# Eight transformer layers on one core: a planned order of short steps, scores computed twice, weights multiplied first

## The chip, the cores and the metric

The kernel runs on one core of a Trainium2 chip. The metric is device time in microseconds (us) for one execution of the whole program. All arithmetic is float32. Five engines matter: PE (TensorE, matmuls; PEld is its weight load), DVE (VectorE), ACT (ScalarE), POOL (GpSimd) and SP (SyncE, which only issues transfers here). Each engine works through its own instructions in order.

## The reference

The input is 8 sequences of 256 tokens with 128 features. Eight residual layers follow each other, each on a layernormed copy of x:

```python
x = x + causal_attention(ln(x))        # 1 head, key size 64: softmax(q k^T / 8) (x w_v1) w_v2
x = x + ffn_relu(ln(x))                # only expert 0 counts; ends in a layernorm of its own
x = x + linear_attention(ln(x))        # (theta phi^T) g / sqrt(128), no softmax; latent size 32
x = x + ffn_relu(ln(x))
x = x + retention(ln(x))               # 16 heads of 8, values of 16, decaying causal mask, gate
x = x + ffn_silu(ln(x))                # hidden 384, weights from int32 times 1/127
x = x + softmax_attention(ln(x))       # 16 heads of 8, weights with a low-rank part, no mask
x = x + ffn_silu(ln(x))
```

A sequence needs no other sequence. In softmax attention each of the 16 heads has scores of 256 x 256, with only 8 numbers in each dot product.

## The kernel before, in words

The 2048 tokens are cut into four groups of 512 (two sequences each), and a group into four tiles of 128 tokens. x stays in SBUF for the whole kernel (tiles `x0` to `x3`). All weights are loaded at the start; those for later layers stand behind x in the SP queue.

Every layer of a group is a Python generator that yields at a few places. A small loop at the end of `hybrid` keeps two layers of two different groups active and advances them in turn; since layers are handed out group by group, the four groups go through one layer two at a time before the next layer begins. The order on an engine is the order in which the generators were advanced, as the tile framework then places it. Buffers come from rotating pools of two to four; PSUM is three pools of two buffers: `ps_two` (two banks each), `ps_one` and `ps_held` (one bank each). A new tile waits until the last user of the buffer's former tile is done.

Places that the change and the prediction touch:

- `layernorm` (L204 to L217): statistics per tile on DVE, variance plus epsilon on DVE (L216), power -0.5 on POOL (L217), four normalisations on DVE (L209). `transposed` (L237, L239): four transposes on PE, one copy out on ACT.
- `causal_attention` (L261 to L313): q, k, v1 projections, value product, scores (L280), exponential (L291), transposes (L299), weighted values (L304 to L308).
- `ffn_relu`: L361 up, L362 and L365 the relu on ACT and DVE, L375 down, L369, L248 and L383 biases and scale on POOL. `ffn_silu`: L598 gate, L599 up, L600 silu, L607 down.
- `linear_attention` (L322 to L345): theta, phi and g projections, then phi^T g, then the product with theta.
- `spread_heads` (L391): one DMA per head moves its 8 rows of q and k to a partition group of 32[...].
- `retention`: projections L437 and L451, chunk scores L470 (64x64 pieces), states L486 to L499, carried part L514, weighted values L522 (64x17 pieces), root on DVE (L222 to L231), gate L551, output L557 to L567. `centre_values` (L185, L186) prepares a weight.
- `softmax_attention`, for each of 64 pairs of heads, in a pipeline of three: `probabilities` with queries as rows (L642), maxima over a row on DVE (L648), four exponentials with the maximum as a bias per row (L654); `turned`, eight transposes (L667) and two copies out (L671), because the next product needs keys as rows; `weighted` (L401), values with a column of ones, which yields the sums as well. After four pairs the result is turned back (L410, L414) and divided (L684, L685).

Of the kernel before, what the change touches and what calls it, by code (L numbers as in the profile page):

```python
# [10 lines left out]

# [25 lines left out]
ONES = 16  # L37
EPS = 1e-5
MASKED = -1e30
PAIRS = [(b, h2) for b in range(2) for h2 in range(HEADS // 2)]  # L40
HEADS_NEXT = "heads"
# [3 lines left out]
def hybrid(ctx: ExitStack, tc: tile.TileContext, t: dict, out: bass.AP):  # L45
    nc = tc.nc

    const = ctx.enter_context(tc.tile_pool(name="const", bufs=1))
    work = ctx.enter_context(tc.tile_pool(name="work", bufs=2))
    work3 = ctx.enter_context(tc.tile_pool(name="work3", bufs=3))  # L50
    small = ctx.enter_context(tc.tile_pool(name="small", bufs=4))
    psum = ctx.enter_context(tc.tile_pool(name="psum", bufs=2, space=bass.MemoryType.PSUM))

    def two_banks():
        return psum.tile([P, 2, N], F32, tag="two", name="ps_two")

    def one_bank():
        return psum.tile([P, N], F32, tag="one", name="ps_one")

    def held_bank():  # L60
        return psum.tile([P, N], F32, tag="held", name="ps_held")


    def load(name, shape, src=None, dtype=F32):
        tl = const.tile(shape, dtype, tag=name, name=f"c_{name}")
        nc.sync.dma_start(tl, t[name] if src is None else src)
        return tl

    def load_row(name, n):

        tl = const.tile([P, n], F32, tag=name, name=f"c_{name}")
        nc.scalar.dma_start(tl, t[name].partition_broadcast(P))
        return tl
# [4 lines left out]
    for g in range(GROUPS):  # L78
        x.append(const.tile([P, NT, D], F32, tag=f"x{g}", name=f"x{g}"))
    nc.sync.dma_start(x[0], x_in[0])  # L80
    w_qkv1 = load("a_qkv1", [P, 3, 64])
    for g in range(1, GROUPS):
        nc.sync.dma_start(x[g], x_in[g])
    w_v2 = load("a_v2", [64, D])
    w1 = load("f_w1", [P, 512])
    w2 = load("f_w2", [P, 4, D], t["f_w2"].rearrange("(c p) d -> p c d", p=P))
    w_tpg = load("b_tpg", [P, 192])
    w_ret_qk = load("r_qk", [P, 4, P])
    rot_tab = load("r_tab", [P, 4, S])
    w_ret_vg = load("r_vg", [P, 512])  # L90
    w_ret_o = load("r_o", [P, 2, D], t["r_o"].rearrange("(c p) d -> p c d", p=P))
# [7 lines left out]
    b1 = const.tile([P, 4], F32, tag="f_b1", name="c_f_b1")  # L99
# [4 lines left out]
    b_ret_qk = const.tile([P, 4], F32, tag="r_qkb", name="c_r_qkb")  # L104
# [6 lines left out]
    ident = const.tile([P, P], F32, tag="ident", name="ident")  # L111
    make_identity(nc, ident)
    minus_half = const.tile([P, 32], F32, tag="mhalf", name="mhalf")
    nc.gpsimd.memset(minus_half, -0.5)

    causal_add = const.tile([P, 3, P], F32, tag="causal_add", name="causal_add")
    nc.gpsimd.memset(causal_add, 0.0)

    causal_mul = const.tile([P, 1, P], F32, tag="causal_mul", name="causal_mul")
    nc.gpsimd.memset(causal_mul, 1.0)  # L120
    for c in (0, 2):
# [4 lines left out]
    nc.gpsimd.affine_select(  # L126
        out=causal_mul[:, 0, :], in_=causal_mul[:, 0, :], compare_op=ALU.is_ge,
        fill=0.0, base=0, pattern=[[1, P]], channel_multiplier=-1,
    )

    chunk_mul = const.tile([P, 64], F32, tag="chunk_mul", name="chunk_mul")
    for e in range(2):
        half = slice(64 * e, 64 * e + 64)
        nc.gpsimd.tensor_copy(chunk_mul[half, :], causal_mul[half, 0, half])
    causal_add = causal_add.rearrange("p a b -> p (a b)")

    own_head = const.tile([P, HEADS, VONE], F32, tag="own_head", name="own_head")
    nc.gpsimd.memset(own_head, 1.0)
    for step, base in ((-KDIM, 0), (KDIM, KDIM - 1)):
        nc.gpsimd.affine_select(  # L140
            out=own_head, in_=own_head, compare_op=ALU.is_ge, fill=0.0, base=base,
            pattern=[[step, HEADS], [0, VONE]], channel_multiplier=1 if base == 0 else -1,
        )


    values32 = []
    for g in range(2):
        values32.append(const.tile([P, NT, HEADS, 32], F32, tag=f"v{g}", name=f"values32_{g}"))
        nc.gpsimd.memset(values32[g], 1.0)


    def dequantised(wi, shape, name):
        w = const.tile(shape, F32, tag=name, name=name)
        nc.vector.tensor_copy(w, wi)
        nc.vector.tensor_scalar_mul(w, w, float(np.float32(1.0 / 127.0)))
        return w

    def prepare_ffn_int():
        return (
            dequantised(wi_gate, [P, 384], "wf_gate"),  # L160
            dequantised(wi_up, [P, 384], "wf_up"),
            dequantised(wi_down, [P, 3, D], "wf_down"),
        )

    def prepare_lora():

        w = w_lora
        ps = one_bank()
        for i in range(3):
            nc.tensor.matmul(  # L170
                ps[:, i * P : (i + 1) * P], lora_a[:, i, :], lora_b[:, i, :], start=True, stop=True
            )
        nc.vector.scalar_tensor_tensor(
            w.rearrange("p i d -> p (i d)"), ps[:, : 3 * P], 2.0,
            w_lora.rearrange("p i d -> p (i d)"), ALU.mult, ALU.add,
        )
        nc.vector.tensor_scalar_mul(w[:, 0, :], w[:, 0, :], float(KDIM**-0.5))
        return w

    def centre_values():  # L180

        for w in (w_ret_vg, b_ret_vg):
            v = w[:, : HEADS * VDIM].rearrange("p (h d) -> p h d", h=HEADS)
            mean = const.tile([P, HEADS], F32, tag="r_mean", name="r_mean")
            nc.vector.tensor_reduce(mean, v, AX.X, ALU.add)  # L185
            nc.vector.scalar_tensor_tensor(  # L186
                v, spread_over(mean, VDIM), -1.0 / VDIM, v, ALU.mult, ALU.add
            )

# [8 lines left out]
    def layernorm(src):  # L198
        stats = small.tile([P, NT, 6], F32, tag="ln_stats", name="ln_stats")
        mv = small.tile([P, NT, 2], F32, tag="ln_mv", name="ln_mv")  # L200
        rstd = small.tile([P, NT], F32, tag="ln_rstd", name="ln_rstd")
        y = work3.tile([P, NT, D], F32, tag="ln_y", name="ln_y")
        for i in range(NT):
            nc.vector.bn_stats(stats[:, i, :], src[:, i, :])  # L204
            nc.vector.bn_aggr(mv[:, i, :], stats[:, i, :])  # L205
        inverse_root(rstd, mv[:, :, 1], 1.0)
        yield
        for i in range(NT):
            nc.vector.tensor_scalar(  # L209
                y[:, i, :], src[:, i, :], mv[:, i, 0:1], rstd[:, i : i + 1], ALU.subtract, ALU.mult  # L210
            )
        return y

    def inverse_root(rstd, var, scale):

        nc.vector.tensor_scalar(rstd, var, scale, EPS, ALU.mult, ALU.add)  # L216
        nc.gpsimd.tensor_tensor(rstd, rstd, minus_half[:, : rstd.shape[1]], ALU.pow)  # L217

    def newton_root(r, a):

        t = small.tile(list(a.shape), F32, tag="root_t", name="root_t")
# [11 lines left out]
    def transposed(y):  # L233

        ps = one_bank()
        for i in range(NT):
            nc.tensor.transpose(ps[:, i * P : (i + 1) * P], y[:, i, :], ident)  # L237
        yT = work3.tile([P, N], F32, tag="yT", name="yT")
        nc.scalar.copy(yT, ps)  # L239
        yield  # L240
        return yT

    def normalised(g):
        y = yield from layernorm(x[g])
        return (yield from transposed(y))

    def add_row_to(g, row):
        nc.gpsimd.tensor_tensor(x[g], x[g], tokens(row, NT), ALU.add)  # L248

    def add_to(g, tiles, ps):  # L250
        xs = flat(x[g][:, tiles, :])
        nc.vector.tensor_tensor(xs, ps, xs, ALU.add)  # L252


    def causal_attention(g):
        yT = yield from normalised(g)
        qk = work.tile([64, 2, N], F32, tag="a_qk", name="a_qk")
        v1T = work.tile([64, N], F32, tag="a_v1T", name="a_v1T")
        ps = two_banks()
        for i in range(2):  # L260
            nc.tensor.matmul(ps[:64, i, :], w_qkv1[:, i, :], yT, start=True, stop=True)  # L261
        nc.vector.tensor_copy(qk, ps[:64])
        ps = one_bank()
        nc.tensor.matmul(ps[:64, :], w_qkv1[:, 2, :], yT, start=True, stop=True)
        nc.scalar.copy(v1T, ps[:64, :])
        yield
        values = work.tile([P, NT, D], F32, tag="values", name="a_values")
        ps = one_bank()
        for i in range(NT):
            nc.tensor.matmul(  # L270
                ps[:, i * P : (i + 1) * P], v1T[:, i * P : (i + 1) * P], w_v2, start=True, stop=True
            )
        nc.scalar.copy(flat(values), ps)
        yield
        for b in range(2):
            at = b * S
            blocks = ((0, 0, P), (P, P, 3 * P))
            ps = one_bank()
            for q0, lo, hi in blocks:
                nc.tensor.matmul(  # L280
                    ps[:, lo:hi], qk[:, 0, at + q0 : at + q0 + P], qk[:, 1, at : at + hi - lo],
                    start=True, stop=True,
                )
# [308 lines left out]
    def ffn_silu(g, w_gate, w_up, w_down):  # L592
        yT = yield from normalised(g)
        hT = work.tile([P, 3, N], F32, tag="hT", name="g_hT")
        for c in range(3):
# [6 lines left out]
            if c > 0:  # L602
                yield
# [238 lines left out]
```

## Time and profile before

| | |
|---|---|
| time, median of 3 runs | 765.78 us (765.4 to 773.27) |
| span in the profile | 772.2 us, 12437 instructions |
| granted TensorE clock, mean | 0.829 |
| transfers | 10.49 MB, mean 14 GB/s |

| stage, by the chain of waits | us from the start |
|---|---|
| loads, first layernorms | 0 to 19 |
| causal attention | 19 to 72 |
| feed-forward (relu) | 72 to 129 |
| linear attention | 129 to 152 |
| feed-forward (relu) | 152 to 213 |
| retention | 213 to 422 |
| feed-forward (silu), softmax attention, feed-forward (silu) | 422 to 772 |

The profile page lists busy time per engine, then forty equal slices of the span with the busy share in tenths, then the chain of work that ended last, followed back from the last instruction. Groups of instructions have a line, an engine, an operation, output<-input, sizes, count, busy time and mean duration of one, then the idle time ahead of them and what ended it. "Clock" is the share of PE's full clock that the chip granted. These are the costliest groups:

```profile
L654 ACT ACTIVATE l_p<-ps_two,l_nmax 128x256 f32<-128x256 f32 x256 | 100.5, 475 | 108.1 <-DVE l_nmax L648 108.1
L648 DVE TENSOR_REDUCE l_nmax<-ps_two 128x4 f32<-128x1024 f32 x64 | 78.3, 1223 | 41.1 <-PE ps_two L642 40.1
L217 POOL TENSOR_TENSOR ln_rstd<-ln_rstd,mhalf 128x4 f32<-128x4 f32 x40 | 40.6, 1016 | 415.8 <-DVE ln_rstd L216 415.8
L671 DVE COPY l_pT<-ps_held 128x512 f32<-128x512 f32 x128 | 82.6, 676 | 9.3 <-PE ps_held L667 9.2
L642 PE MATMUL ps_two<-spread 8*128 8x256 f32 x512 | 79.4, 404 | 0.3 <-DMA spread<-qk 0.3
L667 PE MATMUL ps_held<-ident,l_p 128*128 128x128 f32 x512 | 74.6, 282 | 0.8 <-ACT l_p L654 0.8
```

### The profile page before, as it was taken

Reading aid. Unit: us, or ns where it says so; the run is one execution under the profiler, and the core shown is the slowest. Engines: PE = TensorE matmul, PEld = TensorE weight load, DVE = VectorE, ACT = ScalarE, POOL = GpSimd, SP = SyncE. Lnnn points to the kernel's source line nnn. Section 1 sums busy time; section 2 is a strip of 40 time slices with the busy share of each in tenths; the row PEclk is TensorE's granted clock in tenths of the full one; section 3 lists DMA queues with packets and bytes.
Section 4 is the critical chain, followed back from the end, with each engine's and each line's share of the span. In section 5 each row is a group of like instructions: output and inputs, shape, how many; then the busy total and the mean of one; then the engine's idle time right before and its main releaser. Section 6 shows DMA issues by size and latency. Waiting matters only on the chain.

```text
span 772.2 us, 12437 instructions
## 1 busy us (share of the span) xinstructions
PE 653.3 (85%) x5038; PEld 421.3 (55%) x5038; DVE 436.2 (56%) x1120; ACT 215.7 (28%) x468; POOL 108.1 (14%) x107
## 2 busy tenths in 40 slices
PE   0989574984588979989889978999999999999985
PEld 0556443662433865655556655666666666565653
DVE  3662546645583445434533455588688688766542
ACT  0333120221010011100100222544454454456541
POOL 5021233324251010110110022100000000000000
PEclk9875867995876556757655899899999999999997
DMA  7000000000003000010010000210010010000000
GB/s 227 4 1 0 1 0 1 1 0 0 1 10 45 3 1 2 12 18 2 12 18 2 2 0 1 40 16 1 1 28 2 1 28 1 1 14 1 15 14 14
DMA packets 10232, 10.49 MB, mean 14 GB/s; under 512 B 1776, under 2 KB 8512, under 8 KB 10176
## 3 DMA queue, kind: packets, MB, share of 16 engines
q1 hardware_dynamic: 9024, 9.11, 5.9%
q10 hardware_dynamic: 1152, 0.59, 0.4%
q8 instruction: 40, 0.66, 0.3%
q14 instruction: 16, 0.13, 0.1%
HBM read 4.45 MB, written 1.05 MB: 7 GB/s over the span
## 4 chain that ended last, share of the span: by engine, by line
PE 72%; DVE 15%; POOL 5%; ACT 3%; DMA 2%; issue 2%; POOLq 0%; ACTq 0%; SPq 0%; DVEq 0%
PE ps_two L642 9%; PE ps_one L401 8%; PE ps_held L667 8%; PE ps_held L522 5%; PE ps_two L361 4%; PE ps_one L495 4%; PE ps_two L470 3%; DVE ln_y L209 3%; POOL ln_rstd L217 3%; PE ps_one L607 2%; PE ps_one L237 2%; PE ps_two L598 2%; PE ps_two L437 2%; PE ps_two L599 2%; PE ps_one L375 2%; PE ps_one L567 2%
## 5 line engine op out<-in xcount | busy, mean ns | idle before, releaser
L654 ACT ACTIVATE l_p<-ps_two,l_nmax 128x256 f32<-128x256 f32 x256 | 100.5, 475 | 108.1 <-DVE l_nmax L648 108.1
L648 DVE TENSOR_REDUCE l_nmax<-ps_two 128x4 f32<-128x1024 f32 x64 | 78.3, 1223 | 41.1 <-PE ps_two L642 40.1
L217 POOL TENSOR_TENSOR ln_rstd<-ln_rstd,mhalf 128x4 f32<-128x4 f32 x40 | 40.6, 1016 | 415.8 <-DVE ln_rstd L216 415.8
L237 PE MATMUL ps_one<-ident,ln_y 128*128 128x128 f32 x128 | 31.3, 377 | 71.6 <-DVE ln_mv L205 42.3
L671 DVE COPY l_pT<-ps_held 128x512 f32<-128x512 f32 x128 | 82.6, 676 | 9.3 <-PE ps_held L667 9.2
L642 PE MATMUL ps_two<-spread 8*128 8x256 f32 x512 | 79.4, 404 | 0.3 <-DMA spread<-qk 0.3
L667 PE MATMUL ps_held<-ident,l_p 128*128 128x128 f32 x512 | 74.6, 282 | 0.8 <-ACT l_p L654 0.8
L401 PE MATMUL ps_one<-l_pT,values 128*32 128x256 f32 x512 | 73.3, 385 | 0.0
L667 PEld LDWEIGHTS ps_held<-ident,l_p 128*128 128x128 f32 x512 | 56.9, 142 | 24.0 <-ACT l_p L654 13.6
L237 PEld LDWEIGHTS ps_one<-ident,ln_y 128*128 128x128 f32 x128 | 19.9, 176 | 84.3 <-issue 54.7
L642 PEld LDWEIGHTS ps_two<-spread 8*128 8x128 f32 x512 | 48.3, 185 | 26.8 <-issue 20.3
L239 ACT COPY yT<-ps_one 128x512 f32<-128x512 f32 x32 | 18.8, 587 | 137.5 <-PE ps_one L237 137.3
L209 DVE TENSOR_SCALAR ln_y<-x,ln_mv,ln_rstd 128x128 f32<-128x128 f32 x128 | 45.2, 398 | 20.7 <-POOL ln_rstd L217 20.6
L522 PEld LDWEIGHTS ps_held<-values,r_s 64*64 64x64 f32 x1024 | 46.4, 188 | 6.0 <-issue 5.2
L522 PE MATMUL ps_held<-values,r_s 64*64 64x17 f32 x1024 | 48.0, 243 | 0.0
L252 DVE TENSOR_TENSOR x<-ps_one,x 128x256 f32<-128x256 f32 (+1 forms) x28 | 15.0, 536 | 48.2 <-PE ps_one L567 21.5
L470 PEld LDWEIGHTS ps_two<-spread 8*64 8x64 f32 x1024 | 27.9, 187 | 26.3 <-issue 19.1
L401 PEld LDWEIGHTS ps_one<-l_pT,values 128*32 128x32 f32 x512 | 27.4, 109 | 26.3 <-issue 12.7
L470 PE MATMUL ps_two<-spread 8*64 8x64 f32 x1024 | 35.6, 290 | 5.0 <-DVE r_s L475 5.0
L495 PE MATMUL ps_one<-values,r_k 64*128 64x272 f32 (+1 forms) x64 | 33.2, 640 | 4.0 <-ACT r_k L488 4.0
L204 DVE BATCH_NORM_STATS2 ln_stats<-x 128x6 f32<-128x128 f32 x128 | 31.7, 272 | 7.9 <-DMA x<-in_x 7.6
L361 PE MATMUL ps_two<-yT,c_f_w 128*128 128x512 f32 x64 | 34.4, 690 | 0.0
(144 smaller groups left out, 893.9 us busy)
## 6 DMA issues: line engine op xcount, KB each, us to landing
spread<-qk SPq DMA_DIRECT2D x128, 32.0 KB
x<-in_x SPq DMA_DIRECT2D x4, 256.0 KB
out<-x SPq DMA_DIRECT2D x4, 256.0 KB
c_f_w<-in_f_w SPq DMA_DIRECT2D x2, 256.0 KB
c_r_tab<-in_r_tab SPq DMA_DIRECT2D x1, 512.0 KB
c_r_vgb<-in_r_vgb ACTq DMA_DIRECT2D x1, 256.0 KB
c_r_qk<-in_r_qk SPq DMA_DIRECT2D x1, 256.0 KB
c_r_vg<-in_r_vg SPq DMA_DIRECT2D x1, 256.0 KB
```

The lines of the kernel that those rows point to most:

```text
L209: nc.vector.tensor_scalar(y[:, i, :], src[:, i, :], mv[:, i, 0:1], rstd[:, i : i + 1], ALU.subtract, ALU.mult)
L237: nc.tensor.transpose(ps[:, i * P : (i + 1) * P], y[:, i, :], ident)
L361: nc.tensor.matmul(ps[:, k, :], w1[:, c * P : (c + 1) * P], yT, start=True, stop=True)
L401: nc.tensor.matmul(o[32 * i : 32 * (i + 1), (j % 2 + 1) * S - weights.shape[1] : (j % 2 + 1) * S], v, weights, start=(n == 0), stop=(n == ...
L470: nc.tensor.matmul(ps[64 * e : 64 * e + 64, k, 64 * jt : 64 * jt + 64], heads[rows, jt // 2, 1, at : at + 64], heads[rows, jt // 2, 0, at ...
L495: nc.tensor.matmul(ps[:, : HEADS * VONE], k[:rows, m, :], v[:rows, 2 * b + m, :, :VONE], start=(c == 0), stop=(c == len(pieces) - 1),)
L522: nc.tensor.matmul(ps[half, VONE * h : VONE * (h + 1)], s[half, h % 4, h // 4 * 2 + m, :], v[half, 2 * b + m, h, :VONE], start=alone, stop ...
L642: nc.tensor.matmul(ps[:, k, m * S : (m + 1) * S], qk[rows, j, 0, at + m * P : at + (m + 1) * P], qk[rows, j, 1, at : at + S], start=True, ...
L648: nc.vector.tensor_reduce(nmax, ps.rearrange("p k (m s) -> p (k m) s", m=2), AX.X, ALU.max, negate=True)
L654: nc.scalar.activation(p[:, k, m * S : (m + 1) * S], ps[:, k, m * S : (m + 1) * S], AF.Exp, bias=nmax[:, 2 * k + m : 2 * k + m + 1],)
L667: nc.tensor.transpose(ps[:, c * S + m * P : c * S + (m + 1) * P], p[:, k, m * S + c * P : m * S + (c + 1) * P], ident,)
L671: nc.vector.tensor_copy(flat(pT[:, 2 * k : 2 * k + 2, :]), ps)
```

## The change

**Threads and a plan.** Each group is one thread that runs through all eight layers; inside a layer it spawns further threads for independent parts. A thread asks for buffers from stores (8 PSUM banks, 31 work buffers and some others), names steps ("this engine, this many us"), and emits the instructions of a step when its turn comes. A planner inside the kernel walks through these steps at build time with the durations written in the kernel, gives each engine the earliest step that can start (the lower group first where several can), and so fixes the order of each engine and the use of each buffer. The framework then keeps that order (`manual_schedule`). Some copies, normalisations and relus may go to ACT or DVE, whichever the plan finds free first.

**Scores twice.** Instead of turning the probabilities, the kernel computes the scores a second time with keys as rows. The maximum of each query enters the second product as a ninth row of the operands (the maximum on the query side, ones on the key side), so that one exponential covers a pair of heads without a bias, and its result feeds the weighted values as it is. The maxima get there by a transpose, a copy and a DMA. The first scores of one pair and the second of another are issued together, where possible on four different row groups.

**Weights multiplied first.** W_q W_k^T and W_v1 W_v2 are made once, as is the product of phi and theta; linear attention then starts from y^T y.

**Smaller edits.** Layernorm computes a shift beside the root on POOL, so that ACT can normalise; heads are stored so that one DMA moves four of them; retention's states come from chunks of 64, summed on POOL; the int weights are converted in place; the output leaves in halves.

Core of the diff (lines that are only "..." mark what is left out):

```diff
-    def turned(p):
-        pT = work.tile([P, 4, S], F32, tag="l_pT", name="l_pT")
-        for k in range(2):
-            ps = held_bank()
-            for c in range(2):
-                for m in range(2):
-                    nc.tensor.transpose(...)
-            nc.vector.tensor_copy(flat(pT[:, 2 * k : 2 * k + 2, :]), ps)
-        return pT
...
+    def pairs_of_scores():
...
+            yield step(PE, 0.9)
+            for n in range(2):
+                for k in range(2):
+                    if one:
+                        seq, h2 = one
+                        rows, j = place(2 * h2 + k)
+                        nc.tensor.matmul(
+                            ps1[:, k, n * S : (n + 1) * S],
+                            seq.spread[rows, j, 0, n * P : (n + 1) * P],
+                            seq.spread[rows, j, 1, :], start=True, stop=True,
+                        )
+                    if two:
+                        seq, h2 = two
+                        rows, j = place(2 * h2 + k)
+                        nc.tensor.matmul(
+                            ps2[:, k, n * S : (n + 1) * S],
+                            seq.spread[rows, j, 1, n * P : (n + 1) * P],
+                            seq.spread[rows, j, 0, :], start=True, stop=True,
+                        )
...
+    def maxima(seq, h2, ps):
...
+        for j in range(2):
+            yield step(SP, 0.5)
+            nc.sync.dma_start(
+                seq.spread[KDIM:P:32, 2 * half + j, 0, :], rows[8 * j : 8 * j + 8, :]
+            )
...
+    def exponentials(seq, h2, ps):
+        p = yield get(probs)
+        yield step(ACT, 1.05, "exp")
+        nc.scalar.activation(flat(p), flat(ps), AF.Exp)
...
     def layernorm(src, y):
...
-        inverse_root(rstd, mv[:, :, 1], 1.0)
+        yield step(POOL, 1.5)
+        nc.gpsimd.tensor_scalar(rstd, mv[:, :, 1], EPS, None, ALU.add)
+        nc.gpsimd.tensor_scalar(shift, mv[:, :, 0], -1.0, None, ALU.mult)
+        nc.gpsimd.tensor_tensor(rstd, rstd, minus_half, ALU.pow)
+        nc.gpsimd.tensor_tensor(shift, shift, rstd, ALU.mult)
...
+    for g in range(GROUPS):
+        plan.start(layers(g), g, 4.0 + 1.5 * g)
...
+    plan.run()
...
-        hybrid(tc, t, out)
+        with tc.manual_schedule():
+            hybrid(tc, t, out)
```

## The prediction

> **What bounds the kernel now.** I read the engine totals and the slices first, then the chain of waits, then the chain in the softmax stage, then the timeline of the start.
>
> ```profile
> PE 653.3 (85%) x5038; PEld 421.3 (55%) x5038; DVE 436.2 (56%) x1120; ACT 215.7 (28%) x468; POOL 108.1 (14%) x107
> PE   0989574984588979989889978999999999999985
> PEclk9875867995876556757655899899999999999997
> PE 72%; DVE 15%; POOL 5%; ACT 3%; DMA 2%; issue 2%; POOLq 0%; ACTq 0%; SPq 0%; DVEq 0%
> ```
> TensorE carries 72% of the chain. From 480 us on it is busy in nearly every slice; between 213 and 422 us (retention) it is busy at a low clock; before that it has gaps.
>
> ```profile
> 501.12 1.07 PE ps_two L642 x8
> 502.19 1.02 PE ps_held L667 x8
> 503.22 0.99 PE ps_one L401 x8
> 504.21 1.07 PE ps_two L642 x8
> ```
> This is the chain in the softmax stage, nothing but TensorE. One pair of heads costs 504.21-501.12 = 3.09 us: scores, transposes, weighted values. 64 pairs: 198 us. (A float32 matmul is two instructions here, a transpose one.)
>
> ```profile
> 266.33 3.53 PE ps_held L522 x64
> 433.87 1.97 PE ps_held L522 x64
> 238.00:300.00 62.00, 55.74 (x654) 38.71 (x653) 20.20 (x58) 5.62 (x14) 3.59 (x3) 0.51 0.07 11
> 494.00:560.00 66.00, 65.82 (x486) 41.86 (x484) 50.40 (x81) 31.65 (x78) 1.02 (x1) 1.00 0.07 10
> 72.00:129.00 57.00, 35.74 (x176) 23.89 (x174) 28.55 (x106) 7.84 (x12) 18.61 (x16) 0.80 0.00 1
> ```
> The same 64 instructions of retention take 3.53 us at the half clock and 1.97 at the full one. The windows (busy PE, PEld, DVE, ACT, POOL; clock last but two) show retention's core at 0.51, softmax at 1.00 and 99.7% busy, and the first feed-forward layer only 63% busy on TensorE: two groups at a time do not hide a layernorm's chain DVE-POOL-DVE-PE-ACT there.
>
> ```profile
> 17.56 0.42 DVE L185 TENSOR_REDUCE r_mean<-c_r_vg 128x16 f32<-128x256 f32 x1 [4.03 <-DMA c_r_vg<-in_r_vg]
> 19.20 2.27 PE L237 MATMUL ps_one<-ident,ln_y 128*128 128x128 f32 x8 [19.20 <-DVE ln_y L209]
> ```
> TensorE starts at 19.2 us because VectorE, in order, waits for a late weight of retention ahead of the first normalisation.
>
> [...] The trace has two side by side: a 512-column matmul costs 0.86 us (chain: L437 x4 in 1.73), so four 256-column ones in series would be 1.72; L642's eight instructions take 1.07. Four at once it does not show. [...] Here 4 x 0.216 = 0.86 of the 1.07 is streaming, so I charge 0.2 us a change. [...]
>
> **The change part by part**, with instruction counts from the built order of the changed kernel.
>
> *Softmax.* Per pair it drops 8 transposes (1.02 us PE), two 128x512 evictions on DVE (L671: 128 x 676 ns = 83 us in all), and turns four exponentials of 128x256 (475 ns each, 100.5 us in all) into one of 128x1024; the nearest row is Silu L457, 1058 ns, so 64 x 1.06 = 68 us. It adds a second score product per pair, keys as rows. First and second scores of different pairs are issued together, over four row groups where both are at hand. The built order has 39 such double steps, 25 with first scores alone and 25 with second alone: 89 steps. A double step has twice the instructions over twice the row groups, so I take the measured 1.07 us for each kind: 89 x 1.07 = 95 us. Bounds: with no gain from four groups a double step costs 0.86 more, 34 us in all. Weighted values go over four column groups instead of two: 32 blocks of 16 instructions at the 0.99 us of L401's eight = 32 us (60 if they gain nothing). So 127 us against 198. The maximum travels to the second product through a transpose, a copy and one DMA (32 in all; chain: "483.38 2.40 DMA spread<-qk"). Since TensorE runs in order, a late row holds all matmuls queued behind it, those of other groups too; I put 0 to 1 us on each, 0 to 32, and take 0 because the order leaves other steps between.
>
> *Weights multiplied first.* Causal attention loses two of its three 512-column projections per group, and the 64x1024 copy (1.21 us); linear attention works on y'y. About 10 us less on PE, contained in the counts below.
>
> *Layernorm.* The DVE step L216 (7.1 us) goes; 107 of 160 normalisations move to ACT; POOL has four instructions instead of one (pow 1.02 us; the others I take at 0.1 to 0.2, from memsets of 0.1), so the POOL leg grows from 1.0 to about 1.5 us: 40 times, but hidden where three other groups run.
>
> *TensorE's sum, at full clock.* 124 matmuls of 512 columns x 0.865 = 107. 390 of 128 columns x 0.224 (L375 x32 in 3.59) = 87, and 8 of 256, 3. 296 transposes x 0.128 (L667 x8 in 1.02) = 38. Retention's small ones: scores 16 x 1.91 = 31; weighted values 16 x between 1.97 and 3.53, I take 2.75, = 44; states and carried parts 48 matmuls x 0.63 (L495 x4 in 1.32; L514 x2 in 0.60) = 30. Softmax 127. The built order changes tile shape 255 times, of which 121 are inside the softmax prices; 134 x 0.2 = 27. Sum 494 us, against 653 busy before.
>
> *The other engines*, at before's durations: DVE keeps the statistics (64) and the maxima (78) and has about 90 in retention; all rows together 343 us instead of 436. ACT rises to about 250, with 22 table loads x 1.28 instead of 16. POOL 141. None reaches TensorE, so these edits cost nothing where TensorE has work queued.
>
> *Threads.* Four groups instead of two are interleaved in steps, over 8 PSUM banks and 31 work buffers held singly. So one group's layernorm lies beside another's matmuls. Before, TensorE was busy 652.5 of the 753 us after its start, 87%, with 99.7% in the softmax stage and 63% in the worst. I take 94%: 494/0.94 = 526 us. The retention weights no longer stand in front of the first normalisation; x[0] is there at 3.71 us and ACT is free of its DMA issues at 8.2, so TensorE starts near 9 us instead of 19. The end needs about 4 us after the last matmul, as now. 526 + 9 + 4 = 539, say 540 us.
>
> **Rivals.**
>
> A. Narrow tiles gain nothing from four groups, and retention, now spread over more of the span, drags the rest into the half clock. PE 494 + 34 + 28 + 13 (weighted values all cold) + 25 (a tenth of the 250 us of wide matmuls and transposes cold) = 594; at 92% 646 + 13 = 659. For it: clock 0.51 over retention's core though TensorE is 90% busy there. Against: [...] softmax at clock 1.00 with 8-row matmuls.
>
> B. Retention runs beside dense work and stays warm (weighted values 32 us, states 20): 494 - 22 = 472, at 97% 487 + 9 + 4 = 500. For it: 99.7% in softmax before with only two groups. Against: the first 100 us of TensorE's work (causal, linear, feed-forward) have as much on DVE, by my sum 104 us, so TensorE cannot be full there.
>
> C. The frozen order is wrong. It rests on durations fixed in the kernel; where TensorE is at half clock or a DMA late, each engine waits in order and the waits spread. At the fill of the worst window, 63%: 494/0.63 + 13 = 797, slower than before. For it: 32 DMAs on the path of the scores, every engine in order. Against: the stage with an unmixed, steady order filled TensorE[...].
>
> **How the numbers follow.** The main case 0.60, A 0.15, B 0.20, C 0.05. The time is the main case's, 540. The range reaches down past B, to 470 (468 of PE work at 100% would be about there), and up to 640, most of the way to A; outside lie C and about half of A on one side and a little of B on the other. Even A is faster by 14%: faster 0.95, same 0.01, slower 0.04.
>
> **What would show it.** Right: PE busy near 490; a double score step at about 1.1 us for 16 instructions in the chain; no transposes of probabilities; DVE near 343 with L671's copies gone; first matmul near 9 us; clock above 0.85; the chain still led by PE. Wrong: double steps near 1.9 us or clock below 0.75 (A); PE waits on the rows' DMA, or PE fill below 80% with waits spread over all engines (C); DVE at over 85% of the span would mean that I priced the evictions or the normalisations too low.

## The result: 568 us, and the profile after

| | before | changed |
|---|---|---|
| time, median of 4 runs each | 768.75 us | 568.1 us (559.82 to 572.31) |
| ratio | | 0.7329, 95% interval 0.7213 to 0.7445 |
| span in the profile | 772.2 us | 565.8 us |
| PE busy, and without work | 653.3, 118.9 us | 506.0, 59.8 us |
| granted TensorE clock, mean | 0.829 | 0.891 |

The ratios here and below leave the slower runs of a kernel out, so they need not be the quotient of the medians, and the profiles of the paired steps and of the third twin are of such slower runs. The forecast was 540 us, range 470 to 640; the time lies inside, 28 us above the forecast. Of the 206 us that the span lost, 147 are work and 59 idle time of TensorE. No run separates saved work from the higher clock in the 147; as an estimate, busy time times mean clock falls from 653.3 x 0.829 = 542 to 506.0 x 0.891 = 451, so some 90 us would be saved work.

The page of the changed kernel, in the same places as before: totals, slices and the engines of the chain.

```profile
PE 506.0 (89%) x5020; PEld 333.5 (59%) x5020; DVE 328.9 (58%) x877; ACT 242.1 (43%) x426; POOL 150.6 (27%) x250
PE   2899979989999979999999999999898989677757
PEclk9999979969799698999999999995999687768768
PE 75%; DVE 12%; ACT 6%; issue 2%; DMA 2%; POOL 1%; ACTq 0%; POOLq 0%; DVEq 0%
```

TensorE does almost the same number of instructions (5020 for 5038) in 147 us less. Read the slices from both ends: from the second on they are 7 to 9, where before the first third fell to 4 and 5. The last six fall to 5 to 7, and the clock is 6 to 8 in the last nine. Before, the end was the best part; now it is the worst.

The costliest groups, those that stand against the ones shown of before:

```profile
L1035 DVE TENSOR_REDUCE small<-twin 128x4 f32<-128x1024 f32 x64 | 78.1, 1220 | 46.4 <-PE twin L1015 33.5
L1066 ACT ACTIVATE probs<-twin 128x1024 f32<-128x1024 f32 x64 | 65.5, 1023 | 77.3 <-PE twin L1015 77.0
L1082 PE MATMUL bank<-probs,l_values 128*32 128x256 f32 x512 | 40.1, 456 | 0.2 <-ACT probs L1066 0.2
L843 PE MATMUL bank<-r_values,work 64*64 64x17 f32 x768 | 30.0, 216 | 0.0
```

The maximum costs what it did (1220 ns, before 1223). One exponential of 1023 ns stands for four of 475, the transposes and their copies are gone, and the weighted values take 40.1 us instead of 73.3. L843 are retention's weighted values (another 256 write a twin).

The timeline of TensorE shows a double step of scores: start, duration, instruction.

```profile
320.28 0.48 PE L1007 MATMUL twin<-l_spread 32*128 32x256 f32 x1
320.29 0.48 PE L1015 MATMUL twin<-l_spread 32*128 32x256 f32 x1
320.30 0.48 PE L1007 MATMUL twin<-l_spread 32*128 32x256 f32 x1
320.30 0.48 PE L1015 MATMUL twin<-l_spread 32*128 32x256 f32 x1
320.60 0.37 PE L1007 MATMUL twin<-l_spread 32*128 32x256 f32 x1
...
321.36 1.13 PE L939 MATMUL bank<-work,c_g_gate 128*128 128x512 f32 x2
```

Four instructions, two of the first product (L1007) and two of the second (L1015), start within 0.02 us of each other; the next four follow at 320.60. The sixteen of the step are out of the way in 321.36 - 320.28 = 1.08 us, at a clock of 1.00. Before, eight took 1.07. That four row groups cost no more than two was my estimate in the prediction; here it is measured. As an estimate, eight 256-column products in series would be 8 x 0.43 = 3.46 us (half of the 0.865 us of a 512-column one each), so the step takes 3.2 times less.

The windows of the changed kernel (busy PE, PEld, DVE, ACT, POOL; clock last but two) tell a full stretch from the end:

```profile
300.00:350.00 50.00, 48.82 (x487) 29.11 (x485) 35.75 (x77) 33.22 (x42) 10.25 (x17) 1.00 0.11 18
400.00:450.00 50.00, 46.40 (x386) 28.81 (x385) 23.82 (x50) 27.12 (x33) 5.85 (x10) 0.86 0.03 7
450.00:500.00 50.00, 39.76 (x238) 22.66 (x236) 19.66 (x31) 13.62 (x21) 1.66 (x4) 0.77 0.10 17
500.00:566.00 66.00, 46.39 (x330) 25.25 (x326) 14.76 (x32) 20.69 (x26) 1.66 (x4) 0.76 0.02 5
```

In the last 166 us TensorE works 132.5 us (80%), at a clock of 0.79; it idles 33.5 us there, more than half of the 59.8. No other engine is busy for even 55% of any of these last three windows. What it waits for stands in the chain there, and in the list of PE's waits (us in total, times, the longest):

```profile
482.07 1.09 PE twin L1007 x8
483.18 1.24 DVE small L1035
484.46 1.16 PE twin L1007 x8
485.64 1.24 DVE small L1035
```

```profile
PE twin L1007 <- DVE small L1035: 14.7, 14, 2.2
PE bank L488 <- ACT work L469: 8.3, 5, 4.5
PE twin L1015 <- ACT probs L1066: 7.0, 7, 1.2
```

PE and DVE take turns: a score product, its maximum, and only then the next product, 2.4 us a turn, of which PE works 1.1. A `twin` is a pair of PSUM banks, and the changed kernel has one twin for first scores and one for second scores. While DVE reads the one, PE has nowhere to put the next product of its kind. In the middle of the kernel that time is filled with other layers; at the end little else is left (retention's L843 and L777 ended before 400 us, and the last feed-forward layers fill only part of the time). The last 25 us are something else again: the softmax is over, one group's closing layernorm and feed-forward stand alone, and TensorE idles 11.1 us of them.

### The profile page after: what moved, and what is told of

Read it like the earlier page. It is cut to its first block, busy times and chain, and to the rows that moved or that the text cites. A ratio compares the mean times of both kernels' runs of the same rounds, so it can differ in the third digit from the quotient of the medians.

```text
span 565.8 us, 12205 instructions
## 1 busy us (share of the span) xinstructions
PE 506.0 (89%) x5020; PEld 333.5 (59%) x5020; DVE 328.9 (58%) x877; ACT 242.1 (43%) x426; POOL 150.6 (27%) x250
## 4 chain that ended last, share of the span: by engine, by line
PE 75%; DVE 12%; ACT 6%; issue 2%; DMA 2%; POOL 1%; ACTq 0%; POOLq 0%; DVEq 0%
PE twin L1007 12%; PE twin L1015 7%; PE bank L1082 7%; PE bank L843 5%; DVE small L1035 4%; PE bank L954 3%; PE bank L939 3%; PE bank L660 3%; PE bank L777 2%; PE bank L936 2%; PE bank L515 2%; PE bank L737 2%; ACT probs L1066 2%; PE twin L843 2%; PE bank L488 2%
## 5 line engine op out<-in xcount | busy, mean ns | idle before, releaser
L1035 DVE TENSOR_REDUCE small<-twin 128x4 f32<-128x1024 f32 x64 | 78.1, 1220 | 46.4 <-PE twin L1015 33.5
L1066 ACT ACTIVATE probs<-twin 128x1024 f32<-128x1024 f32 x64 | 65.5, 1023 | 77.3 <-PE twin L1015 77.0
L1007 PE MATMUL twin<-l_spread 32*128 32x256 f32 x512 | 82.7, 438 | 14.7 <-DVE small L1035 14.7
L1015 PE MATMUL twin<-l_spread 32*128 32x256 f32 x512 | 83.1, 446 | 7.0 <-ACT probs L1066 7.0
L460 POOL TENSOR_SCALAR small<-small 128x4 f32<-128x4 f32 x40 | 9.8, 244 | 247.6 <-DVE small L458 239.7
L1007 PEld LDWEIGHTS twin<-l_spread 32*128 32x128 f32 x512 | 49.9, 203 | 41.3 <-DVE small L1035 22.4
L362 ACT COPY work<-bank 128x512 f32<-128x512 f32 (+3 forms) x68 | 34.3, 506 | 64.0 <-PE bank L1082 20.1
L1015 PEld LDWEIGHTS twin<-l_spread 32*128 32x128 f32 x512 | 49.9, 206 | 17.6 <-ACT probs L1066 10.9
L469 ACT ACTIVATE work<-x,small 128x128 f32<-128x128 f32 x84 | 35.8, 484 | 41.9 <-POOL small L463 41.9
L462 POOL TENSOR_TENSOR small<-small,mhalf 128x4 f32<-128x4 f32 x40 | 41.8, 1046 | 0.0
L1082 PE MATMUL bank<-probs,l_values 128*32 128x256 f32 x512 | 40.1, 456 | 0.2 <-ACT probs L1066 0.2
L457 DVE BATCH_NORM_STATS2 small<-x 128x6 f32<-128x128 f32 x128 | 34.3, 268 | 8.7 <-DMA x<-in_x 8.5
L843 PEld LDWEIGHTS bank<-r_values,work 64*64 64x64 f32 x768 | 27.3, 146 | 9.0 <-issue 8.8
L843 PE MATMUL bank<-r_values,work 64*64 64x17 f32 x768 | 30.0, 216 | 0.0
L1082 PEld LDWEIGHTS bank<-probs,l_values 128*32 128x32 f32 x512 | 16.9, 128 | 20.8 <-issue 12.6
L488 PE MATMUL bank<-ident,work 128*128 128x128 f32 x88 | 18.6, 333 | 10.8 <-ACT work L469 8.3
L474 DVE TENSOR_SCALAR work<-x,small 128x128 f32<-128x128 f32 x44 | 19.5, 550 | 8.7 <-POOL small L462 8.6
L939 PE MATMUL bank<-work,c_g_gate 128*128 128x512 f32 x40 | 24.5, 709 | 0.0
```

The source lines that it names most:

```text
L362: (nc.scalar.copy if e == ACT else nc.vector.tensor_copy)(dst, src)
L462: nc.gpsimd.tensor_tensor(rstd, rstd, minus_half, ALU.pow)
L469: nc.scalar.activation(y[:, i, :], src[:, i, :], AF.Identity, bias=shift[:, i : i + 1], scale=rstd[:, i : i + 1],)
L843: nc.tensor.matmul(ps[half, VONE * h : VONE * (h + 1)], s[h % 4][half, at : at + 64], v[half, m, VONE * h : VONE * (h + 1)], start=alone, ...
L939: nc.tensor.matmul(ps[0], w_gate[:, cols], yT[:, :N], start=True, stop=True)
L1007: nc.tensor.matmul(ps1[:, k, n * S : (n + 1) * S], seq.spread[rows, j, 0, n * P : (n + 1) * P], seq.spread[rows, j, 1, :], start=True, sto ...
```

## Experiments

Ratios are to the kernel before in the same call, whose median was 773 to 776 us; the changed kernel's is 0.7329 [0.7213, 0.7445]. A hundredth is 7.7 us. Line numbers in a variant can be some lines off those of the changed kernel. The experiments undo parts one at a time; their costs overlap and are not to be added. No run undoes the product of phi and theta, the smaller edits, or the planned order by itself.

**The old softmax in the new threads** (scores once, four exponentials with a bias, eight transposes, two copies):

```diff
-        nc.scalar.activation(flat(p), flat(ps), AF.Exp)
+        for k in range(2):
+            for m in range(2):
+                nc.scalar.activation(p[...], ps[...], AF.Exp, bias=nmax[...])
...
+                    nc.tensor.transpose(to[...], p[...], ident)
+            yield from copied(pT[:, k, :], to, 0.6)
```

> One part undone: threads, plan and products of weights stay, but softmax attention again computes scores once, with four exponentials per pair and the maximum as a bias, eight transposes and two copies out per pair. Theory (TensorE work over fill): per pair 1.07 + 1.02 and per two pairs 0.99 us, 165 us instead of 127, so PE busy about 545 instead of 506, DVE about 400, and the time rises by about 40, to 590 to 620. Rival (the threads alone made the gain, the second score product only moves work): within 10 us of 568.

Measured 619.38 us, 0.8026 [0.7958, 0.8093]; PE 550.7 us busy, still 89% of the span, clock 0.909.

```profile
PE 550.7 (89%) x5004; PEld 371.1 (60%) x5004; DVE 373.0 (60%) x941; ACT 318.6 (52%) x677; POOL 149.6 (24%) x249
```

Scores twice are worth 0.07, some 54 us, and the gain is TensorE's own work: 44.7 us less of it at the same fill. DVE and ACT get 44 and 76 us more as well, but neither is the bound. The run compares the two forms each with its buffers: here both twins serve the one kind of scores, whose product L994 never waits (0.0 us of idle ahead of it, where the changed kernel's L1007 has 14.7).

**Two groups at a time.** The first thread runs group 0 and then 2, the second 1 and then 3:

```diff
-    for g in range(GROUPS):
-        plan.start(layers(g), g, 4.0 + 1.5 * g)
+    def chain(g):
+        yield from layers(g)
+        yield from layers(g + 2)
+
+    for g in range(2):
+        plan.start(chain(g), g, 4.0 + 1.5 * g)
```

> One part undone: only two of the four groups run side by side; the third follows the first in the same thread, the fourth the second. All instructions stay. Theory (four groups fill TensorE where a layernorm or a softmax of one waits): PE busy stays near 506, fill drops, time 620 to 680, with the loss all over the span. Rival (the order within a group's steps does it, two are enough, as the old softmax stage with 99.7% suggests): below 585.

Measured 686.25 to 714.34 us over four runs (no interval), the profiled span 685.2: even the fastest run is about 120 us above the changed kernel, more than expected. PE is busy for 80% of the span and, at a clock of 0.840, needs 545.0 us for the same instructions. Its waits in this run:

```profile
PE bank L488 <- ACT work L469: 34.0, 13, 9.2
PE twin L1007 <- DVE small L1035: 25.5, 25, 2.2
```

The layernorm's leg costs 34.0 us of waits instead of 8.3. Undone alone, the width of the interleaving costs more than any saved arithmetic that was undone here.

**All groups with equal rank**, so that they go through the layers abreast instead of spread out over them:

```diff
-            plan.current.rank = min(a[0].g for a in (one, two) if a)
...
-        plan.start(layers(g), g, 4.0 + 1.5 * g)
+        plan.start(layers(g), 0, 4.0 + 1.5 * g)
```

> All groups get the same priority in the plan, so that they move together instead of the first running ahead. Theory (what is lost against the forecast is the last third, where one or two groups are left and TensorE waits for the single twin of each kind): the end is fuller, 545 to 560, mean clock above 0.9. Rival (mixing of different layers is what fills TensorE; groups in step all want VectorE or all TensorE): 575 or more, with gaps spread over the whole span.

Measured 616.26 us, 0.7889 [0.7817, 0.7960]. PE's work is unchanged (507.7 us) and fills 83% of the span instead of 89%; the wait for the maxima more than doubles:

```profile
PE twin L1006 <- DVE small L1034: 33.2, 31, 1.5
```

In its trace retention's scores (L777) end before 300 us and the first softmax product begins after it, while in the changed kernel both run between 200 and 400 us. So it isn't enough to have four threads: they must stand in different layers, so that the softmax of one has other layers' matmuls beside it.

**Single steps**, first and second scores never issued together:

```diff
-            if seconds:
+            if seconds and not one:
```

> First and second scores are never issued together: 128 steps over two row groups each instead of 39 double and 50 single ones. Theory (four row groups stream at once, a double step costs as a single one): 39 more steps x 1.07 = 42 us more on PE; part of it falls into the idle time of the last third, so 585 to 610. Rival (four row groups share one stream, a double step is worth two single ones): 568 within 6 us.

Measured 668.65 us, 0.8647 [0.8577, 0.8717]: 102 us more than the changed kernel, far above the expected 585 to 610. There are 39 more steps, 39 x 1.08 = 42 us. PE is busy 66 us longer (572.0), so some 24 us go into slower instructions, and it idles 31 us longer, 27 of them after 400 us. (The edit also makes second scores wait until no first ones are at hand, so the order changes with it.) In the end of the kernel the chain looks so for long stretches:

```profile
545.31 2.10 PE twin L1007 x8
547.43 1.24 DVE small L1035
548.71 2.10 PE twin L1007 x8
550.84 1.24 DVE small L1035
```

The same eight instructions take 2.10 us, not 1.06, and the turns are longer by that. The changed kernel's trace shows both at their clocks: 1.06 us at 292.74 with 1.00 granted, 2.00 us at 212.41 with 0.50. From 450 us to the end of this run PE is busy 159.6 of 213 us, at a clock of 0.70 to 0.77 in four windows. Whether the waits bring the half clock is tried below, with the third twin and with added matmuls.

**More double steps**: a first product waits for a second one while rows of maxima are under way, 60 double steps and 8 single instead of 39 and 50:

```diff
+            if firsts and not seconds and todo["rows"]:
+                yield until(lambda: seconds)
             one = firsts.popleft() if firsts else None
```

> First scores are held back while the rows of maxima of an earlier half are on their way, so that nearly all steps are double: 60 double and 8 single ones instead of 39 and 50. Nothing else changes. Theory (a double step costs TensorE what a single one costs, and TensorE is the bound): 21 steps fewer x 1.07 = 22 us less, 540 to 555, PE busy about 485. Rival (each step has only one twin of each kind, so that a double step must wait for VectorE and ScalarE both; holding back adds the trip of the maxima to the path): 568 or more.

Measured 573.41 us, 0.7356 [0.7253, 0.7459], no difference from the changed kernel. PE's work falls by 18.5 us to 487.5, and all of it comes back as waits:

```profile
PE twin L1011 <- DVE small L1039: 26.4, 23, 2.0
PE twin L1019 <- DMA l_spread<-small: 4.3, 3, 3.0
```

**A third twin** once the last sequence of a group has begun: two of the single banks form it, and both kinds of scores take any of the three.

```diff
-    twins = [psum.tile(...) for i in range(2)]
+    twins = [psum.tile(...) for i in range(3)]
+    third = [twins[2][:, k, :] for k in range(2)]
...
+            if not grown and todo["started"] >= TAIL:
...
+                home[:] = [any_twin, any_twin]
```

> When the last sequence has its heads spread, two of the four single banks become a third twin, and the three twins serve both kinds of steps, so that TensorE can start a step while VectorE or ScalarE still reads the one before. Theory (the last 100 us are lost because TensorE, one twin and VectorE take turns): TensorE's waits on the maxima and exponentials there, 21.7 us in the changed kernel, mostly go, 545 to 560. Rival (at the end one group is left and its chain is as long as it is, whatever the buffers): 563 to 573.

Measured 553.75 us, 0.7158 [0.7072, 0.7243]. PE's two waits of the softmax shrink from 14.7 and 7.0 us to 4.9 and 3.3, and the clock after 450 us rises from 0.77 and 0.76 in its two windows to 0.84 (450 to 500 us) and 0.82 (500 to 560):

```profile
PE twin L1021 <- DVE small L1051: 4.9, 5, 2.2
PE twin L1029 <- ACT probs L1084: 3.3, 5, 1.2
```

**Matmuls that nobody needs**, 22 of 128x512, one in each step of scores once at most two sequences are left:

```diff
+            if todo["sequences"] <= 2:
+                yield step(PE, 0.86)
+                nc.tensor.matmul(spare, ident, w1, start=True, stop=True)
```

> Work is added: once only the last two sequences are left in softmax attention, each of its 22 score steps is followed by one 128x512 matmul into a spare bank that nobody reads (0.86 us at full clock, 19 us in all). Theory (in the last third TensorE's gaps bring the half clock, and the half clock then doubles the steps on the path): the dummies fall where TensorE waits for the maxima anyway and hold the clock, the clock of the last 80 us rises from 0.8 to above 0.95, and the time does not grow by 19 us but falls to 545 to 565. Rival (the half clock costs nothing, since VectorE sets the pace there): 575 to 590.

Measured 560.87 us, 0.7176 [0.7096, 0.7255]. In the windows of this run the end is at nearly the full clock:

```profile
450.00:500.00 50.00, 45.90 (x325) 24.82 (x329) 22.48 (x34) 16.26 (x25) 1.66 (x4) 1.00 0.11 17
500.00:560.00 60.00, 42.35 (x281) 21.90 (x273) 11.85 (x28) 16.89 (x21) 1.66 (x4) 0.90 0.02 6
```

PE is busy 503.4 us, of which the additions are at least 22 x 0.86 = 19; the needed work takes at most 484 instead of 506, and the softmax's two waits shrink to 5.3 and 2.7 us. Work was added and the time fell, by 0.017 or 13 us against the run with another stagger in the same call (next), and the clock between 450 and 500 us is 1.00 where the changed kernel has 0.77: so the half clock of the end costs more than what was added beside it. No long gap of TensorE goes with the half clock: between 400 and 541 us of the changed kernel no idle stretch is longer than 2.2 us, and the clock is 0.80. Nor does the busy share of a profile tell the clock: retention's core before was 90% busy (55.74 of 62 us) at 0.51. What it is that sets the clock, these runs don't show.

**The same code with another stagger**, as a measure of what a new plan does by chance, in the same call as the run above:

```diff
-        plan.start(layers(g), g, 4.0 + 1.5 * g)
+        plan.start(layers(g), g, 4.0 + 2.0 * g)
```

> Only the plan's starting times change: the groups enter 2.0 instead of 1.5 us apart. No instruction is added or removed; another order comes out. It measures how far a new plan alone moves the time. Theory: within 1.5% of 568, 560 to 577. Rival (the order is luck, one plan among many that differ by several per cent): off by more than 10 us, which would explain that taking back the product of causal weights cost 24 us with 11 us more work on TensorE.

Measured 566.48 us, 0.7346 [0.7296, 0.7395]. This other plan moves nothing, though it is one of many. The intervals of the third twin and of the added matmuls lie below this one; both overlap the wide one of the changed kernel's own runs.

**Both aids at once**:

> The changed kernel with both aids at once: a third twin from the last sequence of a group on (two of the single banks), and 22 matmuls of 128x512 that compute nothing needed, each in a bank of the plan, once at most two sequences are left. Theory (the end loses time for two reasons that add up: turns between PE and the vector engines for want of a twin, and the half clock that the gaps bring): the twin took 14 us and the added matmuls 7 us, so 540 to 552 us, with the clock of the last 100 us above 0.9. Rival (both work on the same idle time, which the twin has filled already, and each added matmul takes a bank that the last group needs): 553 to 570 us, at or above the run with the third twin alone.

Measured 556.87 us, 0.7176 [0.7145, 0.7206]: below the changed kernel's interval, and no better than either aid alone. The windows of the end:

```profile
450.00:500.00 50.00, 47.19 (x310) 25.47 (x306) 21.33 (x34) 17.41 (x26) 2.92 (x5) 0.97 0.11 17
500.00:560.00 60.00, 48.02 (x342) 25.05 (x334) 14.15 (x31) 19.95 (x26) 1.66 (x4) 0.90 0.02 6
```

Between 450 and 500 us PE is 94% busy at a clock of 0.97, so little of either loss is left there, but the additions, 19 us in all, are of no use. The time is the rival's: the two gains don't add up. Whether waits and half clock are one loss seen twice, or the additions use up what the twin frees, isn't told apart. Of the 18.4 us that PE still idles after 400 us, 11.0 lie in the last 24, the closing feed-forward, which neither aid touches.

**Paired steps and the third twin together:**

> First scores are held back for double steps (60 double, 8 single) and the third twin is there for the last sequence. Theory (fewer steps save TensorE 19 us of work, but each needs both engines' release; with a third twin at the end the waits shrink): 540 to 555. Rival (double steps wait on two releases with one twin of each kind for most of the span, where the third twin does not exist): 560 to 575, no better than pairing alone.

Measured 582.96 us, 0.7555 [0.7485, 0.7626], worse than either alone, against both theories. PE waits 16.6 us for the maxima and 5.1 us for the rows. Why the third twin doesn't help behind the pairing rule wasn't followed up.

**The causal layer's plain weights** (three projections of 64 and a second value product; the premultiplied weights gone):

```diff
-            nc.tensor.matmul(ps, w[:, 0, :], yT[:, :N], start=True, stop=True)
+            nc.tensor.matmul(ps[:64, :], w_qkv1[:, i, :], yT[:, :N], start=True, stop=True)
...
+            nc.tensor.matmul(ps[:64, :], w_qkv1[:, 2, :], yT[:, :N], start=True, stop=True)
...
+            by_tiles(ps, a_v2, v1T[:64, :])
```

> One part undone: causal attention projects q, k and v1 each and then multiplies v1 by the second value weight, as before the change. Theory (TensorE is the bound, and two 512-column matmuls of 0.86 us per group come back, with two more copies): 7 us more on PE, 572 to 582. Rival (the first layer waits for layernorms and loads, so the work is hidden): within 3 us of 568.

Measured 592.39 us, 0.7664 [0.7588, 0.7741], 26 us more. PE's work rises by 10.7 us where 7 were expected (the prediction's "about 10 us" was for causal and linear attention together); counted in the trace, the plan has 36 double steps of scores for 39, which makes the other 3. The rest of the 26 is waiting, on layernorms (17.8 us for 8.3) and on a product on POOL:

```profile
PE bank L475 <- ACT work L456: 17.8, 4, 8.2
PE bank L884 <- POOL work L877: 6.8, 3, 4.7
```

Whether those waits come from the longer layer itself or from the other order that the planner then makes isn't told apart by this run.

**Without the rows' trip**: the DMA that carries the maxima to the second product is left out, so the second scores are exponentiated without their maximum; the query weights are scaled by 0.001 to keep the exponentials finite. Transpose and copy of the maxima stay.

```diff
-            nc.sync.dma_start(
-                seq.spread[KDIM:P:32, 2 * half + j, 0, :], rows[8 * j : 8 * j + 8, :]
-            )
```

> The maxima are still computed, but their trip (transpose, copy, two DMAs per half) is left out and the query weights are scaled by 0.001, so that the exponentials stay finite without a maximum; the second scores follow the maxima on VectorE at once. Theory (the trip lies beside other work, save at the very end): at most 10 us faster, 558 to 570. Rival (matmuls queue on TensorE behind late rows, up to 32 us by the forecast's bound): 545 or less.

Measured 554.77 us, 0.7089 [0.6994, 0.7184], about 19 us by the ratio. The list of PE's waits in the changed kernel holds no wait for these rows; without the trip PE is busy 489.1 us for 506.0, at a clock of 0.916 for 0.891. The plan then has some 42 double steps for 39, which makes 3 us; the rest goes with the higher clock. How the trip would lower the clock isn't settled: this run changes the plan as well, and the numbers that PE multiplies.

## Why the prediction was right, and where it missed

- **Direction and mechanism: right.** TensorE was the bound and its work fell; a double step at full clock is 1.08 us for the 1.07 forecast; the old softmax back in costs 54 us; two threads instead of four cost 120 us or more. DVE (328.9 against 343), ACT (242 against 250) and POOL (150.6 against 141) came out near their sums and bound nothing for most of the span. ACT's 22 table loads take 1283 ns each in the trace, as before's do.
- **TensorE's sum: 494 forecast, 506.0 measured, +12.** The parts missed by more, in both directions. Retention came out at 80.5 us for the 105 forecast (weighted values L843 39.9 for 44, scores L777 19.4 for 31, states and carried parts L812 and L832 21.2 for 30). The largest part of that is a misreading: the sum is headed "at full clock", but its 1.91 us for 64 instructions of scores comes from a stretch at half clock (0.50 between 250 and 262 us). Before's chain also has them at a clock of 1.00, at 305.67:

```profile
257.24 1.91 PE ps_two L470 x64
305.67 1.16 PE ps_two L470 x64
```

16 x 1.16 = 18.6 us would have met the measured 19.4. The half clock moved to the end instead. The score steps of softmax, 95 in the sum, take 116.9 us of PE's time: the 49 before 400 us 58.6 where 52 were forecast, the 40 after it 58.3 where 43 were. The weighted values of softmax are 40.1 for 32, because the 32 instructions of a block take 3.57 us in the chain at a clock of 0.50 (at 500.18) instead of 1.86 at 1.00 (at 252.47). The 512-column matmuls are 135 us for 107, all lines added; a line's busy time overlaps its neighbours' somewhat, but the feed-forward's L939 takes 0.76 us an instruction after 450 us (clock 0.76), where it takes 0.53 between 200 and 300 (clock 0.97). The 107 was a price at full clock for all of them. These four parts add up to some 33 us too much, so the others must have come out some 21 below; they were not taken apart. Among them are the 27 us for changes of shape: 0.2 us for a change was my estimate, the 1.07 us of L642's eight instructions less 0.86, and no run shows what a change costs. (Two slips change nothing: 128 x 676 ns is 86.5 us, of which 82.6 is the group's busy time, and the 652.5 us of PE before are 653.3.)
- **The fill: mis-sized by as much as the work.** The span is 27 us over the 539 that were summed: 12 are work, 3.5 the start, and 12 idle time in between. At 94% the work leaves 32 us idle, with 9 at the start and 4 at the end 45 or so; measured were 59.8. From 20 to 400 us PE idles 14 us, a fill of 96%, so the guess was too low there. The last 166 us have 80% and 33.5 idle us. I used one fill for a span whose end has little but the softmax's own chain left, and then one group's closing layer (11.1 of the 33.5 idle us). With two twins the softmax's chain is product, maximum or exponential, next product, and the clock beside it was 0.77 and 0.76 in the last two windows. The stage of before that I leaned on, 99.7% full, had two buffers in `ps_two` for a single kind of scores; the changed kernel has one for each kind. That was in the code and I didn't price it. The third twin (0.7158) and the added matmuls (0.7176) each bear out a part of it.
- **Start: 9 us forecast.** The first transpose of x runs at 8.00 us, but PE works only 7.5 of the first 20 us, so the start cost 12.5 us, 3.5 more.
- **The rows' trip: 0 taken, out of 0 to 32.** The run without it gained about 19 us, more than the middle of the bounds, though the changed kernel's list of PE's waits has none on the rows. That the 19 us are the trip's own cost isn't shown.
- **Rival A** (no gain from four row groups, all at half clock) is refuted by the double step of 1.08 us and the mean clock of 0.891. **Rival B** was right on retention's states (21.2 us for 20), half right on its weighted values (39.9, between 44 and 32), and wrong on a fill of 97% to the end. **Rival C** (the frozen order spreads waits) is not seen: PE's fill is 89%, and the waits on the rows are not in its list.
- **Small POOL steps** were put at 0.1 to 0.2 us each and take 203 to 244 ns; the leg (L460 to L463) is 1.82 us from start to end (33.55 to 35.37) instead of 1.5. PE's 8.3 us of waits on the normalisation L469 show that this chain is not always hidden, as I had it.

## What to carry to other kernels

Interleave stages of different kinds, and give the width of the interleaving and the spread over layers at least the attention that goes to saved arithmetic. Then price the end on its own: when the last stage stands alone, count the buffers between its engines, because one buffer of a kind makes them take turns, and look at the clock there: in this end it was 0.77, and elsewhere in the trace the eight instructions of a score product took 1.06 us at 1.00 and 2.00 at 0.50. If TensorE's work is cut and the time doesn't move, look for the same microseconds among its waits, as with the paired steps.

## What the hardware showed that I had not expected

Some operations of VectorE took microseconds, up to 8.1, beside memsets of GpSimd. The normalisation L474 (128x128, SBUF to SBUF) has a median of 344 ns, but its mean over 44 is 550, and one took 2982 ns; in the single-step run one took 8126. The timelines of the changed kernel and of the single-step run show what lay beside it:

```profile
18.46 3.05 DVE L474 TENSOR_SCALAR work<-x,small 128x128 f32<-128x128 f32 x2 [1.18 <-POOL small L462]
18.64 2.73 POOL L382 MEMSET r_spread<- 128x1024 f32 x3
```

```profile
19.46 8.19 DVE L474 TENSOR_SCALAR work<-x,small 128x128 f32<-128x128 f32 x2 [1.18 <-POOL small L462]
19.64 2.73 POOL L382 MEMSET r_spread<- 128x1024 f32 x3
22.31 1.62 POOL L378 MEMSET l_values<- 128x576 f32 x3
23.87 3.64 POOL L382 MEMSET l_spread<- 128x1024 f32 x4
```

In the first, the normalisation ends at 21.51 us, just after three memsets (21.37); in the second at 27.65, just after ten (27.51). In the first, more memsets follow at once (from 21.31 to 25.74), and VectorE works on beside them. Not every operation of VectorE is slower there: two reductions L559 take 0.61 us beside memsets of the changed kernel (at 23.32) as without them (at 35.16). The runs with the third twin, the added matmuls, both of them, the stagger and the pairing have two normalisations in 8.18 us too, and PE then works 15.5 to 16.9 us of the stretch from 20 to 40, against 18.93 in the changed kernel's trace. What holds the normalisation, and why it ends after three memsets in one run and after ten in another, no trace shows. That moving or splitting these memsets would win the time back is argued only; it was not tried.
